# Layer 2's messages as two 12-bit float32r parts instead of three bfloat16 parts, with a newly made order of the work

## The chip, the cores and the metric

The kernel runs on one core of one Trainium2 chip. The metric is the device time in microseconds, the median of several runs. Before the change it is 3668.58 us (three runs, 3664.42 to 3668.93). The profiled execution has a span of 3661.3 us.

## What is computed

Four graph layers in a row work on 64 graphs of 256 nodes with 256 features, and each layer has the form x = x + layer(relu(layernorm(x)), adj). Layer 0 is attention with 8 heads under an adjacency mask, layer 1 a graph attention whose softmax runs over the rows, layer 3 one with 4 heads. Layer 2, in which the change lies, is a gated graph network of three iterations:

```python
A = (adj != 0).astype(x.dtype)
h = x
for i in range(3):
    m = einsum('bnd,de->bne', h, weight[i])
    aggr = einsum('bst,bsd->btd', A, m)
    h = gru_cell(aggr, h, w_ih, w_hh, b_ih, b_hh)
```

Everything is float32. A holds zeros and ones only.

## The kernel before

The graphs are taken in 32 pairs. A tile of a pair has 128 partitions and four token blocks t (graph g = t // 2, half c = t % 2) of 256 features. Transposed, as hT, it has two feature halves o of 512 columns, 256 per graph. Each pair goes through layer0 to layer3, and several pairs are under way at once, so that the softmaxes of one pair (ACT, DVE and transposes through DRAM) lie beside the matmuls of another.

The program order of all engines is made on the host by `Plan`. Each piece of work is a `Task`, added with the engines it may take, its assumed duration, the buffers it reads, writes and claims, and a latency for transfers. `Plan.order` is a list scheduler: of the tasks that are ready it takes the one that could begin first by the assumed durations, and of equal ones the one with the smallest key. Before, the key was made of the pair, times PERIOD, and of one number per layer for PE (ON_PE), for SP (ON_SP) and for all others. A task that may run on several engines (an eviction of PSUM by ACT or DVE, `evict`, lines 316 and 317) gets the one that the scheduler picks. Buffers come from pools (`SLOTS`: number, shape, type, and how many a younger pair has to leave free). The engines then run that fixed order, each in its own queue, with waits where one needs another's result.

Layer 2 (`layer2`) is written for this algebra: the message weight is folded into the input weights of the gates ahead of time (`giT`, line 411), so an iteration first forms the transposed sum aT = h^T A for the pair and then the gates from aT and hT.

- `messages` (before) splits h, which is float32, into three bfloat16 parts. The first is the upper half of h's own bits. L911 and L916 (both DVE, 128x1024) make the two rests, and the next part is again the upper half of each. The product at L929 multiplies each part with the 0/1 mask in bfloat16 (made at L894): 2 feature halves x 2 graphs x 3 parts x 2 token halves = 24 matmuls of 128x128 by 128x256. Two tasks, one per feature half, each fill a PSUM bank, which is evicted into aT.
- `gate` (L951) multiplies whhT with hT and giT with aT, all in float32, 512 columns a matmul. An iteration has, in this order of adding, the two hn gates (whhT alone), the messages, two r gates, two n gates (giT alone) and two z gates.
- Behind the z gates ACT (L1001) and DVE (L1006, L1011) form the new hT. For the next iteration the tokens-first h is made from it: for all pairs but the last by a DVE transpose (L621) and two transfers through DRAM, which leaves it in another order (`mixed`), for the last pair by PE transposes (L1025).

Other lines that are named below: L538 (PE transposes behind a layernorm), L513 and L519 (the normalised x, ACT or DVE), L567 (the products with wv and wo), L675 (those with wq and wk), L695 (scores of layer 0, four heads beside each other in row groups of 32), L745 (its context, in column groups of 32), L801 and L863 (products of layer 1), L1061 and L1113 (products of layer 3, the second in halves of 64 columns), L726 (scalings of the softmax rows, ACT or DVE), L994 (a subtraction on POOL or DVE).

The scheduler assumed 1.38 us for a block of 12 message matmuls and 1.72 us for two gate matmuls.

Of the kernel before, what the change touches and what calls it, by code (L numbers as in the profile page):

```python
# [10 lines left out]
BF = mybir.dt.bfloat16  # L11
I32 = mybir.dt.int32
# [22 lines left out]
class Task:  # L35
    __slots__ = ("pair", "forms", "bufs", "rank", "layer", "before", "after", "waits", "begin", "end", "engine", "latency", "rest", "key", "index")


class Plan:
# [14 lines left out]
    SPARE, GRAIN = 6, 0.001  # L54
# [4 lines left out]
    PERIOD, REST = 896, 0  # L59
    ON_PE = (-1435, -211, 9269, -4344)  # L60
    ON_SP = (6322, 2165, 5264, -1155)
    OTHERS = (224, 368, 701, 3083)

    def __init__(self, slots, spare):
        self.slots, self.spare = slots, spare
        self.pairs = []
        self.layer, self.rank = 0, None
# [4 lines left out]
    def add(self, forms, reads=(), writes=(), latency=0.0, claims=()):  # L72
# [11 lines left out]
        t.layer = self.layer  # L84
# [24 lines left out]

    def order(self):  # L110
# [11 lines left out]
        for t in reversed(every):  # L122
            t.rest = max((x.rest + 0.2 for x in t.after), default=0.0) + min(f[1] for f in t.forms) + t.latency
            base = t.rank[0] * self.PERIOD - t.rest * self.REST + t.rank[1] * 1e-4
            engine = t.forms[0][0]
            t.key = base + (self.ON_PE if engine == "PE" else self.ON_SP if engine == "SP" else self.OTHERS)[t.layer]
# [3 lines left out]
        free = {}  # L130
# [5 lines left out]
        while ready:  # L136
            best = None
            for t in ready:
                start = 0.0
                new = [b.tag for b in t.bufs if b.slot is None]  # L140
                for tag in set(new):
                    n = new.count(tag)
                    have = slots[tag]
                    if len(have) < n + (spares.get(tag, 0) if t.pair != oldest else 0):
                        break
                    start = max(start, have[n - 1][0])
                else:
                    for form in t.forms:
                        engine = form[0]
                        begin = max(start, free.get(engine, 0.0), free.get("port", 0.0) if len(form) > 3 else 0.0)  # L150
                        for x in t.before:
                            hop = self.HOP[x.engine] + (engine == "SP") * self.MARGIN if x.engine != engine else self.SAME[x.engine]
                            begin = max(begin, x.end + hop)
                        back = self.BACK.get(engine, 0.0) if len(t.forms) > 1 else 0.0
                        key = (round((begin + back) / self.GRAIN), t.key, t.index)
                        if best is None or key < best[0]:
                            best = (key, t, form, begin)
            _, t, form, begin = best
            engine, us, do = form[:3]
            ready.remove(t)  # L160
# [26 lines left out]
def tile_adj_preln_d4(  # L187
# [42 lines left out]
        "w4": (28, [P, T * D], FP, 9),  # L230
        "f3": (2, [P, T, E3], FP, 0),
        "mask": (6, [P, T * N], BF, 1),
        "ps": (8, [P, 512], FP, 2),
        "w2": (6, [P, N2], FP, 2),
        "st": (4, [P, T, 6], FP, 1),
        "mv": (4, [P, T, 2], FP, 1),
        "rs": (4, [P, 2, T], FP, 1),
        "mx": (16, [P, H0], FP, 2),
        "zs": (12, [P, H0], FP, 2),
        "rz": (12, [P, H0], FP, 2),  # L240
        "f12": (2, [P, 2, T], FP, 0),
        "rows": (3, [T * H3, P], FP, 0),
        "dst": (4, [P, T, H3], FP, 0),
        "turn": (8, [P, T * N], FP, 0),
        "turn2": (4, [P, N2], FP, 0),
        "row1": (4, [N2], FP, 0),
        "row3": (4, [H3 * N2], FP, 0),
# [62 lines left out]
    TURN = 0.118  # L310
# [168 lines left out]
    def norm_relu_T(xt, p, tokens=False):  # L479

        st, mv, rs = buf("st"), buf("mv"), buf("rs")
# [13 lines left out]
        xn, fine = w4(), plan.layer == 3 and p == B // 2 - 1  # L495
# [35 lines left out]
        for i in range(2):  # L531
# [13 lines left out]
            if tokens:  # L545
                add(evict(N2, dst, src), reads=[ps], writes=[(hT, i)])
            else:
                add(
                    [
                        (A, act(N2), lambda dst=dst, src=src: nc.scalar.activation(dst(), src(), AF.Relu)),  # L550
                        (V, dve(N2), lambda dst=dst, src=src: nc.vector.tensor_scalar_max(dst(), src(), 0.0)),
                    ],
                    reads=[ps], writes=[(hT, i)],
                )
        return (at, hT, xn) if tokens else (at, hT)
# [101 lines left out]
    def layer0(xt, p):  # L657
# [27 lines left out]
        for g in range(2):  # L685
            es, pT, mns = [w4() for hh in range(4)], [w4() for hh in range(4)], [buf("mx") for hh in range(4)]
            for ti in range(2):
# [15 lines left out]
                add((PE, 1.11, scores), reads=[qT, kT], writes=banks, claims=[*es, *mns])  # L703
                for e, b, mn in zip(es, banks, mns):
# [9 lines left out]
                    add((V, 2 * FUSED, logits), reads=[b, mb], writes=[(e, ti), (mn, ti)])  # L714
            for e, eT, mn in zip(es, pT, mns):
# [21 lines left out]
                turn(e, eT)  # L737
            psc = bank()
# [14 lines left out]
            add((PE, 1.93, context), reads=[(v, g), *pT], writes=[psc], claims=[cT])  # L753
# [12 lines left out]
    def to_all(row, src, columns, n, dsts):  # L766
# [3 lines left out]
            (PE, TURN, lambda: nc.tensor.transpose(ps()[0:n, 0:P], columns(), ident)),  # L770
# [16 lines left out]
    def layer1(xt, p):  # L787
# [21 lines left out]
        f1 = buf("w2")  # L809
        to_all(buf("row1"), f12, lambda: f12()[:, 0], T, [f1])  # L810
# [14 lines left out]
        )  # L825
        zs, mx, rz = buf("zs"), buf("mx"), buf("rz")
        for g in range(2):
# [28 lines left out]
            )  # L856
        for g in range(2):
# [32 lines left out]
    def layer2(xt, p):  # L890
        at, hT, h = norm_relu_T(xt, p, tokens=True)
        am = buf("mask")
        add(
            (V, dve2(T * N), lambda: nc.vector.tensor_scalar(am(), at().bitcast(I32), 0.0, None, ALU.not_equal), True),  # L894
            reads=[hT, at], writes=[am],
        )
# [3 lines left out]
        def upper(ap):  # L900
            return ap.bitcast(BF).rearrange("p (i h) -> p i h", h=2)[:, :, 1]

        def chunk_of(ap, mixed, t, o):
            if mixed:
                return upper(ap).rearrange("p (m x) -> p x m", x=2 * T)[:, T * o + t]
            return tok(upper(ap))[:, t, o * P : (o + 1) * P]

        def messages(h):
            rest = [w4(), w4()]
            add(  # L910
                (V, dve(T * N), lambda: nc.vector.tensor_tensor(  # L911
                    rest[0](), h(), upper(h()), ALU.subtract), True),
                reads=[h], writes=[rest[0]],
            )
            add(
                (V, dve(T * N), lambda: nc.vector.tensor_tensor(rest[1](), rest[0](), upper(rest[0]()), ALU.subtract), True),  # L916
                reads=[rest[0]], writes=[rest[1]],
            )
            aT = w4()
            for o in range(2):  # L920
                ps = bank()

                def product(o=o, ps=ps):
                    for g in range(2):
                        for i in range(3):
                            part = (h, *rest)[i]
                            for c in range(2):
                                t = 2 * g + c
                                mm(  # L929
                                    ps()[:, g * N : (g + 1) * N], chunk_of(part(), h.mixed, t, o), tok(am(), N)[:, t, :],  # L930
                                    start=i == 0 and c == 0, stop=i == 2 and c == 1,
                                )

                add((PE, 1.38, product), reads=[h, *rest, am], writes=[ps], claims=[aT])
                add(
                    evict(N2, lambda o=o: at_o(aT, o), ps),
                    reads=[ps], writes=[(aT, o)],
                )
            return aT

        for l in range(NL):
            r, hn, u = w4(), w4(), w4()

# [13 lines left out]
            for o in range(2):  # L957
# [9 lines left out]
                )  # L967
            aT = messages(h)
            both = ((whhT, hT), (giT[:, l], aT))
            for o in range(2):  # L970
# [10 lines left out]
                )  # L981
            for o in range(2):
# [14 lines left out]

            for o in range(2):
# [17 lines left out]
            h = w4()  # L1016
            if by_dma(l, p):
# [22 lines left out]
    def layer3(xt, p):  # L1040
# [15 lines left out]
        for t in range(T):  # L1056
# [10 lines left out]
            )  # L1067
        sd = [w4() for i in range(2)]
# [9 lines left out]
        for g in range(2):  # L1078
            zs, rz = buf("zs"), buf("rz")
# [25 lines left out]
            add((V, 0.18, lambda rz=rz, zs=zs: nc.vector.reciprocal(rz(), zs())), reads=[zs], writes=[rz])  # L1105
            pso, oT = bank(), buf("w2")
# [15 lines left out]
            add((PE, 1.86, product), reads=[*eT, (f, 2 * g), (f, 2 * g + 1)], writes=[pso], claims=[oT])  # L1122
            add(evict(N2, oT, pso), reads=[pso], writes=[oT])
            if not last:
# [47 lines left out]
    for p in range(B // 2):  # L1172
        plan.pair()
        plan.layer, xt = 0, buf("x")
# [6 lines left out]
        if p == 0:  # L1181
            for plan.rank, weights in ((None, weights0), (RANKS[0], weights1), (RANKS[1], weights2), (RANKS[2], weights3)):
                weights()
            plan.rank = None
        for plan.layer, layer in enumerate((layer0, layer1, layer2, layer3)):
            layer(xt, p)
        for g in range(2):
# [40 lines left out]
```

## Time and profile before

| | busy us | share of the span |
|---|---|---|
| PE, matmuls | 3600.6 | 98% |
| PE, weight loads (beside the matmuls) | 2042.1 | 56% |
| DVE | 2951.6 | 81% |
| ACT | 2587.2 | 71% |
| POOL | 428.1 | 12% |

| group | instructions | busy us |
|---|---|---|
| L951 matmuls, both operands | 4608 | 2142.5 |
| L929 matmuls | 2304 | 268.2 |
| L911 and L916, DVE | 192 | 235.7 |
| L894, the mask of layer 2, DVE | 32 | 21.9 |
| L621, DVE transposes for the next iteration | 93 | 192.5 |

In the profile an engine's busy time is the time in which one of its instructions is under way. The records of matmuls overlap, since their ends are modelled, so the distance between the starts of two matmuls is the better measure of what one of them costs. A float32 matmul appears as two records, a bfloat16 one as one record, and every record has its weight load beside it. The idle time before an instruction is given with the engine that ended it. The granted clock of TensorE is 1.00 in the middle of the run.

### The profile page before, as it was taken

Reading aid. Unit: us, or ns where it says so; the run is one execution under the profiler, and the core shown is the slowest. Engines: PE = TensorE matmul, PEld = TensorE weight load, DVE = VectorE, ACT = ScalarE, POOL = GpSimd, SP = SyncE. Lnnn points to the kernel's source line nnn. Section 1 sums busy time; section 2 is a strip of 40 time slices with the busy share of each in tenths; the row PEclk is TensorE's granted clock in tenths of the full one; section 3 lists DMA queues with packets and bytes.
Section 4 is the critical chain, followed back from the end, with each engine's and each line's share of the span. In section 5 each row is a group of like instructions: output and inputs, shape, how many; then the busy total and the mean of one; then the engine's idle time right before and its main releaser. Section 6 shows DMA issues by size and latency. Waiting matters only on the chain.

```text
span 3661.3 us, 55666 instructions
## 1 busy us (share of the span) xinstructions
PE 3600.6 (98%) x16369; PEld 2042.1 (56%) x16369; DVE 2951.6 (81%) x8204; ACT 2587.2 (71%) x6995; POOL 428.1 (12%) x455
## 2 busy tenths in 40 slices
PE   8999999999999999999999999999999999999996
PEld 5655555555555555555555555555555555555553
DVE  7886788888888888888888878888888888788655
ACT  6986566787666777667787667776667776677545
POOL 2000111101111011111011111011110011110100
PEclk9999999999999999999999999999999999999997
DMA  7863567876667866667766567766678666677433
GB/s 223 232 190 98 166 191 196 230 200 190 179 178 198 236 190 183 177 183 212 222 190 177 178 195 220 205 188 180 176 195 236 193 185 172 186 209 223 128 99 104
DMA packets 544144, 687.78 MB, mean 188 GB/s; under 512 B 86112, under 2 KB 463072, under 8 KB 543840
## 3 DMA queue, kind: packets, MB, share of 16 engines
q1 hardware_dynamic: 543840, 684.21, 66.3%
q8 instruction: 131, 2.15, 0.3%
q14 instruction: 173, 1.42, 0.1%
HBM read 394.28 MB, written 281.35 MB: 185 GB/s over the span
## 4 chain that ended last, share of the span: by engine, by line
PE 95%; DVE 2%; ACT 2%; DMA 1%; issue 0%; SPq 0%; POOL 0%; POOLq 0%; DVEq 0%; ACTq 0%
PE ps L951 53%; PE ps L929 7%; PE ps L567 6%; PE ps L675 6%; PE ps L695 4%; PE ps L1113 3%; PE ps L863 3%; PE ps L1061 3%; PE ps L745 3%; PE ps L801 3%; PE ps L538 3%; ACT w L651 1%; PE ps L411 0%; DVE w L602 0%; DVE w L644 0%
## 5 line engine op out<-in xcount | busy, mean ns | idle before, releaser
L951 PE MATMUL ps<-w,whhT 128*128 128x512 f32 x2304 | 1076.2, 596 | 1.4 <-ACT w L316 1.4
L951 PE MATMUL ps<-w,giT 128*128 128x512 f32 x2304 | 1066.3, 594 | 0.0
L651 ACT ACTIVATE w<-w,mx 128x256 f32<-128x256 f32 x1536 | 757.1, 496 | 1.5 <-DVE mx L644 1.5
L951 PEld LDWEIGHTS ps<-w,giT 128*128 128x128 f32 x2304 | 432.5, 190 | 530.6 <-issue 502.1
L951 PEld LDWEIGHTS ps<-w,whhT 128*128 128x128 f32 x2304 | 422.4, 190 | 463.9 <-issue 441.8
L602 DVE STREAM_TRANSPOSE w<-w 128x1024 f32<-128x1024 f32 x380 | 467.7, 1236 | 40.2 <-ACT w L726 29.9
L644 DVE CUSTOM_DVE_ANT_0 w<-ps,mask 128x256 f32<-128x256 f32 x1024 | 376.1, 417 | 44.2 <-PE ps L695 44.1
L316 ACT COPY w<-ps 128x512 f32<-128x512 f32 x547 | 302.7, 579 | 132.7 <-PE ps L929 52.6
L994 POOL TENSOR_TENSOR w<-w,w 128x512 f32<-128x512 f32 x95 | 131.0, 1379 | 1821.4 <-ACT w L989 1403.0
L726 ACT ACTIVATE w<-w,rz 128x256 f32<-128x256 f32 x688 | 299.5, 500 | 15.3 <-DVE rz L719 15.3
L973 ACT ACTIVATE w<-ps,brz 128x512 f32<-128x512 f32 x192 | 130.3, 679 | 252.7 <-PE ps L951 252.7
L513 ACT ACTIVATE w<-x,rs 128x256 f32<-128x256 f32 x394 | 211.2, 595 | 117.0 <-DVE rs L505 116.6
L651 ACT ACTIVATION_READ_ACCUMULATOR w<-w,mx 128x1 f32 x1536 | 290.7, 189 | 0.0
L978 DVE SCALAR_TENSOR_TENSOR w<-w,w 128x512 f32<-128x512 f32 x192 | 132.8, 692 | 181.4 <-ACT w L973 181.2
L929 PEld LDWEIGHTS <-w 128*128 128x128 bf16 x2304 | 246.3, 128 | 43.5 <-issue 28.4
L929 PE MATMUL ps<-mask,w 128*128 128x256 bf16 x2304 | 268.2, 273 | 2.2 <-DVE w L916 2.2
L989 ACT ACTIVATE w<-w,bih_sb 128x512 f32<-128x512 f32 x192 | 135.2, 717 | 166.6 <-DVE w L985 166.4
L1091 ACT ACTIVATE w<-w,f 128x256 f32<-128x256 f32 x512 | 228.5, 499 | 7.7 <-DMA w<-row 7.7
L550 ACT ACTIVATE w<-ps 128x512 f32<-128x512 f32 x187 | 104.3, 595 | 168.8 <-PE ps L538 168.8
L1001 ACT ACTIVATE w<-ps,brz 128x512 f32<-128x512 f32 x192 | 129.2, 673 | 126.7 <-PE ps L951 126.4
L486 DVE BATCH_NORM_STATS2 st<-x 128x6 f32<-128x256 f32 x512 | 189.6, 412 | 10.8 <-DMA x<-in_x_dram 7.4
L644 DVE CUSTOM_DVE_ANT_0 w<-w,mask 128x256 f32<-128x256 f32 x512 | 188.3, 420 | 9.9 <-ACT w L1091 9.9
(113 smaller groups left out, 5118.4 us busy)
## 6 DMA issues: line engine op xcount, KB each, us to landing
turn<-w SPq DMA_DIRECT2D x473, 512.0 KB
w<-turn SPq DMA_DIRECT2D x1892, 128.0 KB
w<-in_adj_dram SPq DMA_DIRECT2D x128, 512.0 KB
w<-row SPq DMA_DIRECT2D x64, 512.0 KB
x<-in_x_dram SPq DMA_DIRECT2D x64, 256.0 KB
out_dram<-x SPq DMA_DIRECT2D x64, 256.0 KB
turn<-w SPq DMA_DIRECT2D x62, 256.0 KB
w<-turn SPq DMA_DIRECT2D x248, 64.0 KB
```

The lines of the kernel that those rows point to most:

```text
L316: (A, act(n), lambda: nc.scalar.copy(dst(), src())),
L486: nc.vector.bn_stats(st()[:, t, :], tok(xt())[:, t, :])
L513: nc.scalar.activation(tok(xn())[:, t, :], tok(xt())[:, t, :], func, bias=rs()[:, 1, t : t + 1], scale=rs()[:, 0, t : t + 1])
L567: mm(ps()[:, c * D : (c + 1) * D], chunk(src, k, 2 * g + c), rhs[:, k, :], start=k == 0, stop=k == 1)
L602: add((V, dve(T * N), lambda: nc.vector.transpose(blocks(), blocks())), writes=[e])
L644: nc.vector.tensor_tensor_reduce(row, src, mask, scale, 3.0e38, ALU.add, ALU.min, mn)
L651: nc.scalar.activation(row(e, r), row(e, r), AF.Exp, bias=mn()[:, r : r + 1], scale=-1.0, accum_out=zs()[:, z0(r) : z0(r) + 1])
L675: mm(ps(), w[:, k, o * P : (o + 1) * P], wide(hT, k), start=k == 0, stop=k == 1)
L726: op(row, row, rz()[:, r : r + 1])
L929: mm(ps()[:, g * N : (g + 1) * N], chunk_of(part(), h.mixed, t, o), tok(am(), N)[:, t, :], start=i == 0 and c == 0, stop=i == 2 and c == 1,)
L951: mm(ps(), w[:, k, c0 : c0 + P], wide(src, k), start=n == 0, stop=n == 2 * len(terms) - 1)
L1091: nc.scalar.activation(dst, src, AF.Prelu, bias=f()[:, t, D + h : D + h + 1], alpha=ALPHA)
```

## The change

Layer 2 splits h into two parts: high, a copy into float32r[...], and low, h minus high, in float32r too. The sum of the two is to be as exact as three bfloat16 parts were. The mask A becomes float32r as well, in one tile per graph. The parts are made per graph, half a tile at a time: high by ACT or DVE, low by DVE. The product is now one task per graph: 2 feature halves x 2 parts x 2 token halves = 8 matmuls of 128x128 by 128x256, 16 for a pair. The scheduler assumes 0.9 us for the block of 8. The tiles come from a pool of their own, "part" (12 of half a w4 tile's size), and other pools change their sizes.

The order of the work is made anew: the keys are now one number for each stage of the program (some 60 stages and kinds of engine), and the scheduler knows four ways in which the PE array is tiled (whole, rows, columns, halves), counts 0.19 us for a change between them, and prefers among equal ones a task that stays in the present tiling. The assumed durations of the tiled products are set to what they take without the change of tiling (scores 1.11 to 0.88, context 1.93 to 1.75, layer 3's product 1.86 to 1.75).

The diff, cut to its core (the settings of plan.stage at each stage, the rest of the keys and the other durations are left out):

```diff
+FR = mybir.dt.float32r
...
-    SPARE, GRAIN = 6, 0.001
+    SPARE, GRAIN = 2, 0.001
...
-    PERIOD, REST = 896, 0
-    ON_PE = (-1435, -211, 9269, -4344)
-    ON_SP = (6322, 2165, 5264, -1155)
-    OTHERS = (224, 368, 701, 3083)
+    PERIOD = 1060
+    KEYS = {
+        ("io", "SP"): -9354, ("w", "SP"): 20782, ("w", "on"): 3959, ("w", "PE"): 40499, ("0n", "on"): 4124,
...
+    SWITCH = 0.19
+    HOLD = (0.00, 0.00, 0.00)
+    MODES = ("full", "rows", "columns", "halves")
...
+            t.key = t.rank[0] * self.PERIOD + t.rank[1] * 1e-4 + self.KEYS.get((t.stage, kind), 0.0)
...
+                    data = max(start, self.data(t, engine))
+                    begin = max(data, free.get(engine, 0.0), free.get("port", 0.0) if len(form) > 3 else 0.0)
+                    at = begin
+                    if engine == "PE":
+                        if t.mode != now:
+                            hold = self.HOLD[self.MODES.index(t.mode) - 1] if t.mode != "full" else 0.0
+                            if hold and tiled[t.mode] < 2:
+                                at = max(at, data + hold)
+                            begin = max(at, free.get("PE", 0.0) + self.SWITCH)
+                        elif t.mode != "full":
+                            key -= 1e6
...
         "x": (5, [P, T * D], FP, 0),
-        "w4": (28, [P, T * D], FP, 9),
+        "w4": (24, [P, T * D], FP, 2),
+        "part": (12, [P, N2], FR, 1),
         "f3": (2, [P, T, E3], FP, 0),
-        "mask": (6, [P, T * N], BF, 1),
+        "mask": (4, [P, T * N], BF, 0),
         "ps": (8, [P, 512], FP, 2),
-        "w2": (6, [P, N2], FP, 2),
-        "st": (4, [P, T, 6], FP, 1),
+        "w2": (4, [P, N2], FP, 2),
+        "st": (4, [P, T, 6], FP, 2),
         "mv": (4, [P, T, 2], FP, 1),
-        "rs": (4, [P, 2, T], FP, 1),
-        "mx": (16, [P, H0], FP, 2),
+        "rs": (4, [P, 2, T], FP, 0),
+        "mx": (16, [P, H0], FP, 3),
         "zs": (12, [P, H0], FP, 2),
-        "rz": (12, [P, H0], FP, 2),
+        "rz": (12, [P, H0], FP, 0),
         "f12": (2, [P, 2, T], FP, 0),
         "rows": (3, [T * H3, P], FP, 0),
-        "dst": (4, [P, T, H3], FP, 0),
-        "turn": (8, [P, T * N], FP, 0),
-        "turn2": (4, [P, N2], FP, 0),
-        "row1": (4, [N2], FP, 0),
-        "row3": (4, [H3 * N2], FP, 0),
+        "dst": (4, [P, T, H3], FP, 3),
+        "turn": (8, [P, T * N], FP, 1),
+        "turn2": (4, [P, N2], FP, 1),
+        "row1": (4, [N2], FP, 2),
+        "row3": (4, [H3 * N2], FP, 3),
...
-                add((PE, 1.11, scores), reads=[qT, kT], writes=banks, claims=[*es, *mns])
+                add((PE, 0.88, scores), reads=[qT, kT], writes=banks, claims=[*es, *mns], mode="rows")
...
-        am = buf("mask")
-        add(
-            (V, dve2(T * N), lambda: nc.vector.tensor_scalar(am(), at().bitcast(I32), 0.0, None, ALU.not_equal), True),
-            reads=[hT, at], writes=[am],
-        )
+        ams = [buf("part") for g in range(2)]
+        for g in range(2):
+            add(
+                (V, dve2(N2), lambda g=g: nc.vector.tensor_scalar(
+                    ams[g](), at()[:, g * N2 : (g + 1) * N2].bitcast(I32), 0.0, None, ALU.not_equal), True),
+                reads=[hT, at], writes=[ams[g]],
+            )
         at_o = lambda b, o: tok(b(), N2)[:, o, :]
 
 
-        def upper(ap):
-            return ap.bitcast(BF).rearrange("p (i h) -> p i h", h=2)[:, :, 1]
-
-        def chunk_of(ap, mixed, t, o):
+        def half_of(h, g):
+            if h.mixed:
+                return h().rearrange("p (x g c) -> p g x c", g=2, c=2)[:, g]
+            return h()[:, g * N2 : (g + 1) * N2].rearrange("p (x c) -> p x c", c=2)
+
+        def chunk_of(ap, mixed, c, o):
             if mixed:
-                return upper(ap).rearrange("p (m x) -> p x m", x=2 * T)[:, T * o + t]
-            return tok(upper(ap))[:, t, o * P : (o + 1) * P]
+                return ap.rearrange("p (m o c) -> p o c m", o=2, c=2)[:, o, c]
+            return ap.rearrange("p (c o m) -> p o c m", c=2, o=2)[:, o, c]
+
+        def pairs_of(ap):
+            return ap.rearrange("p (x c) -> p x c", c=2)
 
         def messages(h):
-            rest = [w4(), w4()]
-            add(
-                (V, dve(T * N), lambda: nc.vector.tensor_tensor(
-                    rest[0](), h(), upper(h()), ALU.subtract), True),
-                reads=[h], writes=[rest[0]],
-            )
-            add(
-                (V, dve(T * N), lambda: nc.vector.tensor_tensor(rest[1](), rest[0](), upper(rest[0]()), ALU.subtract), True),
-                reads=[rest[0]], writes=[rest[1]],
-            )
             aT = w4()
-            for o in range(2):
+            for g in range(2):
+                high, low = buf("part"), buf("part")
+                of = h if h.mixed else (h, g)
+                add(
+                    [
+                        (A, act(N2), lambda g=g, high=high: nc.scalar.copy(pairs_of(high()), half_of(h, g))),
+                        (V, dve(N2), lambda g=g, high=high: nc.vector.tensor_copy(pairs_of(high()), half_of(h, g)), True),
+                    ],
+                    reads=[of], writes=[high], claims=[low],
+                )
+                add(
+                    (V, dve(N2), lambda g=g, high=high, low=low: nc.vector.tensor_tensor(
+                        pairs_of(low()), half_of(h, g), pairs_of(high()).bitcast(FP), ALU.subtract), True),
+                    reads=[of, high], writes=[low],
+                )
                 ps = bank()
 
-                def product(o=o, ps=ps):
-                    for g in range(2):
-                        for i in range(3):
-                            part = (h, *rest)[i]
+                def product(g=g, ps=ps, high=high, low=low):
+                    for o in range(2):
+                        for i, part in enumerate((high, low)):
                             for c in range(2):
-                                t = 2 * g + c
                                 mm(
-                                    ps()[:, g * N : (g + 1) * N], chunk_of(part(), h.mixed, t, o), tok(am(), N)[:, t, :],
-                                    start=i == 0 and c == 0, stop=i == 2 and c == 1,
+                                    ps()[:, o * N : (o + 1) * N], chunk_of(part(), h.mixed, c, o), tok(ams[g](), N)[:, c, :],
+                                    start=i == 0 and c == 0, stop=i == 1 and c == 1,
                                 )
 
-                add((PE, 1.38, product), reads=[h, *rest, am], writes=[ps], claims=[aT])
-                add(
-                    evict(N2, lambda o=o: at_o(aT, o), ps),
-                    reads=[ps], writes=[(aT, o)],
+                add((PE, 0.9, product), reads=[high, low, ams[g]], writes=[ps], claims=[aT])
+                add(
+                    evict(N2, lambda g=g: tok(aT(), N2)[:, :, g * N : (g + 1) * N], lambda ps=ps: tok(ps(), N)),
+                    reads=[ps], writes=[(aT, g)],
```

## The prediction, made before the result was known

> **What bounds the kernel now.** I read the page's busy shares and its chain first.
>
> ```profile
> PE 3600.6 (98%) x16369; PEld 2042.1 (56%) x16369; DVE 2951.6 (81%) x8204; ACT 2587.2 (71%) x6995; POOL 428.1 (12%) x455
> ...
> PE 95%; DVE 2%; ACT 2%; DMA 1%; issue 0%; SPq 0%; POOL 0%; POOLq 0%; DVEq 0%; ACTq 0%
> PE ps L951 53%; PE ps L929 7%; PE ps L567 6%; PE ps L675 6%; PE ps L695 4%; PE ps L1113 3%; PE ps L863 3%; PE ps L1061 3%; PE ps L745 3%; PE ps L801 3%; PE ps L538 3%; ACT w L651 1%; PE ps L411 0%; DVE w L602 0%; DVE w L644 0%
> ```
>
> PE is 95% of the chain, and L929, the line that the change rewrites, is 7% of it by itself. A busy PE can still hide stalls, so next the busy time of the middle of the run (its columns: stretch, length, then PE, PEld, DVE, ACT, POOL busy with counts, granted clock, DMA share, GB/s) and what PE waited for in the same stretch:
>
> ```profile
> 300.00:3400.00 3100.00, 3098.18 (x14014) 1749.86 (x14013) 2547.21 (x7022) 2218.87 (x5999) 373.72 (x390) 1.00 0.68 192
> ```
>
> ```profile
> PE ps L929 <- DVE w L916: 1.6, 2, 0.8
> PE ps L1113 <- DMA w<-turn: 0.2, 1, 0.2
> ```
>
> PE waits 1.8 us in 3100. So a microsecond taken off PE's stream there is a microsecond off the time, and the vector work of the change counts only if it begins to delay PE. All other idle PE time stands at the ends: some 21 us before 300 us and 32 us after 3400 us. Third, the price of one matmul. The ends of matmuls are modelled, so I use the distance between starts, in the timeline of PE:
>
> ```profile
> 1817.89 1.88 PE L951 MATMUL ps<-w,whhT 128*128 128x512 f32 x4
> 1819.61 2.78 PE L929 MATMUL ps<-mask,w 128*128 128x256 bf16 x24
> 1822.23 1.04 PE L538 MATMUL ps<-ident,w 128*128 128x128 f32 x8
> 1823.10 1.88 PE L951 MATMUL ps<-w,whhT 128*128 128x512 f32 x4
> ...
> 1858.02 1.88 PE L951 MATMUL ps<-w,giT 128*128 128x512 f32 x4
> 1859.83 1.15 PE L695 MATMUL ps<-w,w 32*128 32x256 f32 x16
> 1860.91 1.99 PE L951 MATMUL ps<-w,whhT 128*128 128x512 f32 x4
> 1862.73 1.88 PE L951 MATMUL ps<-w,giT 128*128 128x512 f32 x4
> ```
>
> L929: 24 matmuls from 1819.61 to 1822.23, 2.62 us or 109.2 ns each. Its neighbours run at their own pace (L951 429 ns a record), so no time is lost at its borders. L695 shows what a change of the array's tiling costs: the L951 ahead takes 1.81 us, not 1.72, L695 itself 1.08, where 16 in groups of four beside each other at 216 ns are 0.86, and the L951 behind 1.82. That is 0.09 + 0.22 + 0.10 = 0.41 us for two switches, 0.2 each.
>
> [...] the trace's bf16 loads on L929 are 128 ns in the mean, f32 ones 190, so float32r may pay the slow load. [...] L916 takes 1.234 us for 1024, so halving the elements is what helps.
>
> **The change part by part.**
> Matmuls. Before, 24 per layer and pair (2 column halves, 2 graphs, 3 parts, 2 chunks), after, 16 (2 parts), over 3 x 32 = 96 such stages: 2304 to 1536, all of 256 columns. The float32r duration is unknown. Lower bound: 109.2 ns[...]. Upper: 216 ns, what one f32 record of 256 columns takes (L863 in the timeline: 16 in 3.56 us less a switch). I take the lower, for two reasons. [...] And the code's own cost for the block of 8 is 0.9 us, 112.5 ns each, in a table whose other entries fit the trace (1.38 for 12 bf16 against 1.31; 1.72 for a gate's four records against 1.72). Slow weight loads hide: f32 loads of 128 columns keep up with L538's 109 ns pace in the timeline, and behind the last of them a load of 190 ns for L951 begins just 107 ns ahead of its matmul. Saved on the path: 768 x 0.1092 = 83.9 us (with 112.5 ns: 79).
>
> Order. In the new order of instructions PE changes tiling 489 times, against 501: 12 x 0.2 = 2.4 us. The planner now knows this cost but finds little to join.
>
> DVE and ACT. Gone: L911 (117.3), L916 (118.4) and the mask L894 (21.9), 257.6 us of DVE. New: 192 low parts at half of L916's size, 0.69 us (the 128x512 tensor-tensor ops of L994), 132 us; masks of 4 bytes, 64 at 0.35 to 0.6, about 30; high parts, placed in the new order 159 on ACT at 0.58 (copies of 512, L316; 92 us) and 33 on DVE at 0.66 (22 us). The order also moves 53 evictions (35 us), some 36 subtractions of L994 (25 us) and 8 others (6) to DVE and a few scalings away from it (-31). DVE: -257.6 + 184 + 66 - 31 = about -39, 2913 us, 81% of a shorter span; ACT about +97, 75%. Neither lies on the path: DVE already kept pace at 2547 of 3100 us.
>
> The new wait. A product waits for high (ACT, queued among exponentials of 0.5 us) and then low (DVE): 0.58 + 0.69 and hops, where it waited for two DVE ops of 1.23. In the new order I counted the PE work between the release of a product's inputs and the product, with these durations and empty queues: at least 4 us in the middle of the run, mostly over 18. Behind the product the gates of L951 begin with whhT, 1.72 us that need no message, which covers the eviction of 0.58. Of the other edges on PE, those under 1 us of room are as many as before (159 against 144), but a handful in the first half (layer 1's product L863 behind its softmax) come out 1 us short. Before had none short and stalled for 1.8 us; I give 3 us.
>
> Buffers. w4 goes from 28 to 24, mask from 6 to 4, w2 from 6 to 4; 12 half-size parts come. Layer 2 no longer takes two w4 a stage for its rests, so this is even: no cost.
>
> Ends. The new SP order puts ten loads of x (2.6 MB) and some of adj ahead of wq to wo. At the page's 223 GB/s wq lands near 13 us, and before, its first product starts at 9.99: +3 us, partly made up later. At the end the last pair has no other pair beside it, and the hn gates (3.4 us), which stood behind the transposes L1025 and covered part of the message chain, now stand ahead of them: eviction, high and low are bare, 2 us in part. Together +5.
>
> Sum: 3668.6 - 83.9 - 2.4 + 3 + 5 = 3590.
>
> **The rivals.**
> A, float32r streams at f32's pace: 1536 x 216 = 332 us against 252, +80: 3668.6 + 80 - 2 + 5 = 3752, slower. [...] Against: [...] the code's 0.9.
> B, the order becomes the bound: with DVE at 81% and ACT at 75% a late high or low, or a gate whose hT comes three vector ops after the last (0.68 + 0.69 + 0.69, room nearly none in the new order in every second pair), stops PE. One DVE operation of 0.69 us in two of three of the 96 stages is 44 us: 3590 + 44 = 3634, still faster. For it: room fell for the norm's transposes behind layers 0 and 1. Against: the same shares did not stop PE before.
> C, a weight load that shows half: 130 ns each, 200 us against 252, 3622.
>
> **How the numbers follow.** Main case 0.75 (3568 to 3612), A 0.09, B 0.12, C 0.04. Range 3566 to 3640: the main case, B and C; below, the ends' 53 us of idle could shrink by 20. Left out is A and the bad tail of B. Faster 0.88, within 0.2% (7 us) 0.02, slower 0.10, A and an unlucky order.
>
> **What would show it.** The product's group should have 1536 records, 109 to 113 ns between starts, so some 170 us; PE busy about 3515; PE's waits in the middle a few us; L951 unchanged at 429 ns. Starts 216 ns apart, or two records a product, would be A. Waits of L951 or the product on DVE or ACT of tens of us would be B. The first wq product near 13 us and more idle in the last 60 us would confirm the ends.

## The result, and the profile after

The changed kernel takes 3688.74 us (four runs, 3687.54 to 3691.11) against 3666.50 us for the kernel before on the same chips: a ratio of 1.0061, 95% interval 1.0047 to 1.0076. It is 0.6% slower; the forecast was 3590 us, 2% faster, with a range of 3566 to 3640.

First the page of the kernel after: busy times, the start of the chain by engine and line, and the rows of the rewritten product.

```profile
PE 3640.1 (99%) x15601; PEld 2103.4 (57%) x15601; DVE 2898.0 (79%) x8293; ACT 2689.2 (73%) x7161; POOL 393.2 (11%) x419
...
PE 90%; ACT 5%; DMA 2%; DVE 2%; SPq 1%; issue 1%; POOL 0%; DVEq 0%; ACTq 0%
...
L984 PE MATMUL ps<-part,part 128*128 128x256 f32 x1536 | 341.2, 371 | 1.7 <-DVE part L969 0.8
L984 PEld LDWEIGHTS ps<-part,part 128*128 128x128 f32 x1536 | 310.4, 279 | 31.3 <-issue 12.6
```

There are 1536 products, as counted, each one record with one weight load. Still their busy time is 341 us, where the 2304 of before had 268. PE is as busy as ever, so the time did not go into waits. The middle of the run and PE's waits in it (the columns are those of the same stretch above) say the same:

```profile
300.00:3400.00 3100.00, 3095.03 (x13131) 1784.24 (x13130) 2473.35 (x7029) 2284.57 (x6080) 337.68 (x349) 1.00 0.67 189
```

```profile
PE ps L788 <- DMA w<-turn: 2.1, 3, 1.1
PE ps L1007 <- DVE w L1071: 1.9, 2, 1.0
PE ps L577 <- ACT w L552: 0.5, 3, 0.2
PE ps L984 <- ACT part L968: 0.4, 1, 0.4
```

4.9 us of waits in 3100, 1.8 before. So the price of a product it is. Two blocks in the timeline of PE, the first from the first iteration of a pair, the second from a later one:

```profile
952.46 1.04 PE L577 MATMUL ps<-ident,w 128*128 128x128 f32 x8
953.25 1.20 PE L984 MATMUL ps<-part,part 128*128 128x256 f32 x8
954.28 0.27 PE L813 MATMUL ps<-ident,dst 128*16 128x128 f32 x1
...
1834.79 1.88 PE L1007 MATMUL ps<-w,whhT 128*128 128x512 f32 x4
1836.10 4.18 PE L984 MATMUL ps<-part,part 128*128 128x256 f32 x16
1840.21 1.93 PE L788 MATMUL ps<-w,w 128*32 128x256 f32 x32
```

The first block of 8 takes 1.03 us to the next group. In the second, the four gates need 1.72 us, so the 16 products have from 1836.51 to 1840.21, 3.70 us, or 231 ns each. Over the whole trace the median distance between the starts of two neighbouring products is 120 ns in the first iteration and 233 ns in the second and third of the pairs 0 to 30, and the weight loads last 190 and 330 ns. In the last pair it is 120 ns in all three iterations. What differs is the order in which h lies. In the first iteration, and in the whole last pair, it is tokens first as PE and ACT left it, and the 128 columns of a weight load lie side by side. Elsewhere it comes back through DRAM in the `mixed` order, the parts keep that order in pairs, and `chunk_of` takes every fourth value: the columns of a weight load are 16 bytes apart.

The first iteration and the last pair make 544 products, the others 992. By these distances they cost 544 x 0.120 + 992 x 0.233 = 296 us, where those of before cost 2304 x 0.1092 = 252 us: +45 us. PE's listed waits fell from 54.5 us to 42.4 (the ends: 20.6 to 18.4 before 300 us, 32.1 to 19.1 after 3400 us), and 12 changes of tiling fewer are worth 2.4 by the forecast's estimate. Together +30; the profiled spans differ by 26.4 us (3661.3 to 3687.7). The other 4 us fit the granted clock of TensorE, here for the runs before and after:

```profile
core 0: 3661.3 us, clock 0.993
core 0: 3687.7 us, clock 0.996
```

In the stretches where the clock was 0.5, PE was busy for 23 us before and for 16 us after. The transposes of 128 columns (L577) stood 213 ns apart there after the change, in the median, and 109 ns at a clock of 1.00. At half the pace that is a loss of 12 and 8 us, an estimate from the clock records of the two traces.

### The profile page after: what moved, and what is told of

Read it like the earlier page. It is cut to its first block, busy times and chain, and to the rows that moved or that the text cites. A ratio compares the mean times of both kernels' runs of the same rounds, so it can differ in the third digit from the quotient of the medians.

```text
span 3687.7 us, 54450 instructions
## 1 busy us (share of the span) xinstructions
PE 3640.1 (99%) x15601; PEld 2103.4 (57%) x15601; DVE 2898.0 (79%) x8293; ACT 2689.2 (73%) x7161; POOL 393.2 (11%) x419
## 4 chain that ended last, share of the span: by engine, by line
PE 90%; ACT 5%; DMA 2%; DVE 2%; SPq 1%; issue 1%; POOL 0%; DVEq 0%; ACTq 0%
PE ps L1007 50%; PE ps L984 8%; PE ps L715 6%; PE ps L607 6%; PE ps L736 3%; PE ps L1177 3%; PE ps L1122 3%; PE ps L788 3%; PE ps L577 3%; PE ps L844 3%; PE ps L909 2%; ACT w L691 2%; DMA w<-turn 1%; ACT w L768 1%; ACT w L1154 0%
## 5 line engine op out<-in xcount | busy, mean ns | idle before, releaser
L354 ACT COPY w<-ps 128x512 f32<-128x512 f32 x500 | 285.4, 582 | 239.1 <-PE ps L984 81.0
L684 DVE CUSTOM_DVE_ANT_0 w<-ps,mask 128x256 f32<-128x256 f32 x1024 | 366.1, 419 | 63.1 <-PE ps L736 60.6
L984 PE MATMUL ps<-part,part 128*128 128x256 f32 x1536 | 341.2, 371 | 1.7 <-DVE part L969 0.8
L984 PEld LDWEIGHTS ps<-part,part 128*128 128x128 f32 x1536 | 310.4, 279 | 31.3 <-issue 12.6
L768 ACT ACTIVATE w<-w,rz 128x256 f32<-128x256 f32 x740 | 319.1, 499 | 4.7 <-DVE rz L761 4.7
L552 ACT ACTIVATE w<-x,rs 128x256 f32<-128x256 f32 x430 | 227.8, 592 | 89.7 <-DVE rs L544 88.3
L538 POOL TENSOR_SCALAR rs<-mv 128x4 f32<-128x4 f32 x129 | 41.1, 319 | 1738.6 <-DVE mv L527 1184.8
L684 DVE CUSTOM_DVE_ANT_0 w<-w,mask 128x256 f32<-128x256 f32 x512 | 198.0, 426 | 36.1 <-ACT w L1154 36.0
L1017 ACT ACTIVATE w<-ps,bhn 128x512 f32<-128x512 f32 x184 | 125.5, 682 | 121.2 <-PE ps L1007 115.3
L1053 POOL TENSOR_TENSOR w<-w,w 128x512 f32<-128x512 f32 x65 | 84.0, 1293 | 1192.9 <-ACT w L1048 749.5
```

Source lines behind the costliest of these rows:

```text
L354: (A, act(n), lambda: nc.scalar.copy(dst(), src())),
L552: nc.scalar.activation(tok(xn())[:, t, :], tok(xt())[:, t, :], func, bias=rs()[:, 1, t : t + 1], scale=rs()[:, 0, t : t + 1])
L684: nc.vector.tensor_tensor_reduce(row, src, mask, scale, 3.0e38, ALU.add, ALU.min, mn)
L768: op(row, row, rz()[:, r : r + 1])
L984: mm(ps()[:, o * N : (o + 1) * N], chunk_of(part(), h.mixed, c, o), tok(ams[g](), N)[:, c, :], start=i == 0 and c == 0, stop=i == 1 and c ...
```

## Experiments

The theory: a float32r operand whose columns lie 16 bytes apart is read at about half the pace (a load of 330 ns in place of 190), and this shows since the matmul of 256 columns, 120 ns behind the short load, is too short to hide it. The rivals: float32r itself is slow, or the h from DRAM; the stream and not the load; the new order. Up to and including "The operands changed places", every kernel keeps the order of PE's instructions as it is after the change, since no assumed duration is touched.

**Weights side by side.** Only the views through which the parts are written and read differ:

```diff
-                return h().rearrange("p (x g c) -> p g x c", g=2, c=2)[:, g]
-            return h()[:, g * N2 : (g + 1) * N2].rearrange("p (x c) -> p x c", c=2)
+                return h().rearrange("p (m o g c) -> p g c o m", o=2, g=2, c=2)[:, g]
+            return h()[:, g * N2 : (g + 1) * N2].rearrange("p (c o m) -> p c o m", c=2, o=2)
...
-            if mixed:
-                return ap.rearrange("p (m o c) -> p o c m", o=2, c=2)[:, o, c]
             return ap.rearrange("p (c o m) -> p o c m", c=2, o=2)[:, o, c]
...
-            return ap.rearrange("p (x c) -> p x c", c=2)
+            return ap.rearrange("p (c o m) -> p c o m", c=2, o=2)
```

> The two parts are written chunk by chunk, so that the 128 columns of every weight load lie side by side, in the second and third iteration too; the order of the work and all else as after the change. Theory 1 (a float32r weight load whose columns lie 16 bytes apart is slow and shows): all L984 products at 120 ns between starts, weight loads 190 ns, 1024 x 113 = 116 us less, 3689 - 116 = 3573 us, faster than both kernels. Theory 2 (float32r itself, or the token order in which h comes back through DRAM, is slow, not the step of the weights): spacing stays 233 ns in these iterations, 3689 us.

Measured: 3625.05 us, ratio to before 0.9885 (0.9869 to 0.9902), faster than both. The products and their loads, and the two casts, in the groups by line:

```profile
L982 PE MATMUL ps<-part,part 128*128 128x256 f32 x1536 | 238.2, 304 | 9.8 <-DVE part L972 7.7 <-ACT part L966 1.0 <-DVE part L967 0.8
L982 PEld LDWEIGHTS ps<-part,part 128*128 128x128 f32 x1536 | 199.5, 191 | 46.7 <-issue 20.6 <-DVE part L972 11.3 <-DVE mx L684 2.5
L972 DVE TENSOR_TENSOR part<-w,part 128x512 fp32r<-128x512 f32 x192 | 184.6, 987 | 29.6 <-ACT part L966 27.5 <-DMA w<-turn 0.5 <-DMA w<-row 0.3
L966 ACT CAST part<-w 128x512 fp32r<-128x512 f32 x159 | 149.8, 975 | 8.6 <-DMA w<-turn 7.9 <-DMA row<-rows 0.6
```

Loads are 191 ns in the mean and the distance is 120 ns in all iterations: theory 1 holds, and h's way through DRAM is not the cause. But 116 us were expected (112 with the count of 992) and 64 came. PE's busy time fell by 90 us (3640.1 to 3550.4), and its idle time rose by 20 us: the casts, which now pick single values 32 bytes apart out of `mixed`, went from 650 to 975 ns on ACT and from 734 to 987 on DVE, and the product waits for L972, the low part.

**The first iteration 16 bytes apart too.** The parts are written as (m o c) in all iterations.

```diff
-            return ap.rearrange("p (c o m) -> p o c m", c=2, o=2)[:, o, c]
+            return ap.rearrange("p (m o c) -> p o c m", o=2, c=2)[:, o, c]
...
-            return ap.rearrange("p (x c) -> p x c", c=2)
+            return ap.rearrange("p (m o c) -> p c o m", o=2, c=2)
```

> The opposite: the parts are written with 16 bytes between the columns of a weight load in the first iteration too. Theory 1: the 512 products of the first iteration go from 120 to 233 ns, 58 us more, 3747 us. Theory 2: the first iteration's h does not come through DRAM and stays at 120 ns, 3689 us.

Measured: 3770.61 us in one run. All products, those of the last pair too, stand at 233 or 234 ns, and their loads are 328 ns in the mean:

```profile
L982 PEld LDWEIGHTS ps<-part,part 128*128 128x128 f32 x1536 | 373.0, 328 | 31.1 <-issue 9.3 <-ACT w L768 2.3 <-DVE mx L684 2.2
```

The first iteration's h never went through DRAM; giving it the layout gives it the price. The time is 24 us above the 3747 of the estimate; the casts took 1160 and 1178 ns in the mean here, which may be part of it.

**8 bytes apart.** The parts are written as (o m c), so that the two token halves lie side by side and a load takes every second value.

```diff
-                return ap.rearrange("p (m o c) -> p o c m", o=2, c=2)[:, o, c]
+            return ap.rearrange("p (o m c) -> p o c m", o=2, c=2)[:, o, c]
...
-            return ap.rearrange("p (x c) -> p x c", c=2)
+            return ap.rearrange("p (o m c) -> p c o m", o=2, c=2)
```

> The parts are written with 8 bytes between the columns of a weight load, in all three iterations. If the load slows with the step, it is between 190 and 330 ns and the spacing between 120 and 233, near 3630 us; if any gap costs the whole, 233 ns everywhere, 3747 us; if only a large step costs, 120 ns, 3573 us. Theory 2: 3689 us.

Measured: 3627.04 us, 120 ns in all iterations, loads 196 ns. The casts are as slow as with the weights side by side, 998 and 996 ns in the mean. A weight load is hardly longer at 8 bytes (196 ns against 190) and is 140 ns longer at 16 (330 ns).

**512 columns streamed.** The strided weights of the change, with both graphs' masks streamed in each product.

```diff
-                                    ps()[:, o * N : (o + 1) * N], chunk_of(part(), h.mixed, c, o), tok(ams[g](), N)[:, c, :],
+                                    ps(), chunk_of(part(), h.mixed, c, o), ams[g](),
```

> Each message product streams the masks of both graphs, 512 columns in place of 256, into a whole bank (the second feature half overwrites the first, so the sums are not those of the layer). The weights are as after the change. Theory 1 (the weight load sets the pace, the stream is hidden behind it): the strided products stay near 233 ns, the contiguous ones go from 120 to 216 ns, 512 x 96 = 49 us more, 3738 us. If the stream sets the 233 ns: 466 and 240 ns, 300 us more, 3989 us.

Measured: 3759.20 us. Twice the columns take the strided products from 233 to 237 ns and the contiguous ones from 120 to 230 ns, in the median. The block shown above, now with 512 columns:

```profile
1868.21 1.88 PE L1007 MATMUL ps<-w,whhT 128*128 128x512 f32 x4
1869.53 4.32 PE L984 MATMUL ps<-part,part 128*128 128x512 f32 x16
1873.78 1.93 PE L788 MATMUL ps<-w,w 128*32 128x256 f32 x32
```

From 1869.93 to 1873.78 it takes 3.85 us, where it took 3.70 with half the columns. So behind 16-byte weights the stream of 256 columns is hidden altogether (233 ns against 237 with twice the columns), and the load of 330 ns sets the pace. The run also answers the rate of the stream: 230 ns for 512 columns is near twice the 109.2 ns that 256 bfloat16 columns took before. Rival A of the forecast, half that rate, is out.

**Pairs, placed well.** Values are read in pairs, as the change does, and the pair is written whole to where the load takes every second value; in the first iteration the parts stay side by side.

```diff
-                return h().rearrange("p (x g c) -> p g x c", g=2, c=2)[:, g]
+                return h().rearrange("p (m o g c) -> p g m o c", o=2, g=2, c=2)[:, g]
...
-                return ap.rearrange("p (m o c) -> p o c m", o=2, c=2)[:, o, c]
+                return ap.rearrange("p (o m c) -> p o c m", o=2, c=2)[:, o, c]
...
+            if mixed:
+                return ap.rearrange("p (o m c) -> p m o c", o=2, c=2)
             return ap.rearrange("p (x c) -> p x c", c=2)
```

> The parts are read and written in pairs of neighbouring values, as the change does it, but the pairs are placed so that the columns of a weight load lie 8 bytes apart (side by side in the first iteration). Products at 120 ns as with contiguous weights, and casts of 0.65 us on ACT and 0.73 us on DVE as after the change, not the 0.98 and 0.99 us that single values 32 bytes apart took. Theory 1a (what the contiguous version lost against its 3573 us are waits for its slow casts): 3689 less 303 - 190 = 113 us, some 3580 us. Rival 1b (the order has no room whatever the casts take): 3610 to 3625 us as with contiguous weights.

Measured: 3597.73 us, ratio 0.9815 (0.9801 to 0.9830), the fastest of all. In the groups by line:

```profile
L986 PE MATMUL ps<-part,part 128*128 128x256 f32 x1536 | 234.1, 302 | 2.5 <-ACT part L970 1.0 <-DVE part L971 0.8 <-DVE part L976 0.4
L986 PEld LDWEIGHTS ps<-part,part 128*128 128x128 f32 x1536 | 198.6, 194 | 36.6 <-issue 20.7 <-DVE mx L684 2.3 <-ACT part L970 1.8
L976 DVE TENSOR_TENSOR part<-w,part 128x512 fp32r<-128x512 f32 x192 | 135.7, 734 | 16.0 <-ACT part L970 13.6 <-DMA w<-turn 1.6
L970 ACT CAST part<-w 128x512 fp32r<-128x512 f32 x159 | 99.7, 658 | 10.7 <-DMA w<-turn 9.8 <-DMA row<-rows 0.6
```

The same 16 products between the same neighbours as in the timeline above:

```profile
1793.56 1.88 PE L1009 MATMUL ps<-w,whhT 128*128 128x512 f32 x4
1794.87 2.48 PE L986 MATMUL ps<-part,part 128*128 128x256 f32 x16
1797.28 1.93 PE L788 MATMUL ps<-w,w 128*32 128x256 f32 x32
```

From 1795.28 (the gates' start plus 1.72) to 1797.28 is 2.00 us, 125 ns each, where it was 3.70 us. The casts are back at 658 and 734 ns, the product waits 2.5 us for them in place of 9.8, and 27 of the 52 us that the contiguous version lacked are there. So its slow casts did cost time (1a). About 18 us against the 3580 of the estimate are still missing: PE is idle 54 us of 3592.9, 6.5 us more than after the change, and of the 112 us by which the products became cheaper (296 - 184) 101 show in PE's busy time.

**The operands changed places.** The mask is the weight, the parts stream, 16 bytes from column to column where h is mixed.

```diff
-                                    ps()[:, o * N : (o + 1) * N], chunk_of(part(), h.mixed, c, o), tok(ams[g](), N)[:, c, :],
+                                    ps()[:, o * N : (o + 1) * N], tok(ams[g](), N)[:, c, o * P : (o + 1) * P],
+                                    part().rearrange("p (m o c) -> p c o m", o=2, c=2)[:, c] if h.mixed else tok(part(), N)[:, c],
```

> The two operands of the message product change places: the mask, whose columns lie side by side, is loaded as weights, and the parts, 16 bytes from column to column in two of three iterations, stream (the sums come out untransposed, so the result is not the layer's). Theory 1 (the step costs only in the weight load): 120 ns everywhere, 3600 us or less. If a stream with 16-byte steps is slowed as the load is: 233 ns in these iterations, 3689 us.

Measured: 3699.46 us; 120 ns in the first iteration, 233 ns in the others, while the weight loads are back at 201 ns in the mean. The same block and the loads:

```profile
1844.22 1.88 PE L1008 MATMUL ps<-w,whhT 128*128 128x512 f32 x4
1845.54 4.29 PE L984 MATMUL ps<-part,part 128*128 128x256 f32 x16
1849.76 1.93 PE L788 MATMUL ps<-w,w 128*32 128x256 f32 x32
```

```profile
L984 PEld LDWEIGHTS ps<-part,part 128*128 128x128 f32 x1536 | 270.8, 201 | 55.4 <-issue 21.0
```

My theory that the step costs only in the load was wrong: a stream of 256 such columns is as slow. Two more runs with other columns of the same tiles followed:

```diff
-                                    part().rearrange("p (m o c) -> p c o m", o=2, c=2)[:, c] if h.mixed else tok(part(), N)[:, c],
+                                    part().rearrange("p (x c) -> p c x", c=2)[:, c] if h.mixed else tok(part(), N)[:, c],
```

> Mask as weights, parts streaming, as in the swapped kernel, but the stream reads the columns 8 bytes apart in two of three iterations (the same tile, other columns; the sums come out untransposed). If 8 bytes cost a stream as little as they cost a weight load: 120 ns everywhere and some 100 us less than the 3699 us of the stream with 16-byte steps, 3600 us. If a stream slows at any gap: 233 ns, 3699 us.

```diff
-                                    part().rearrange("p (m o c) -> p c o m", o=2, c=2)[:, c] if h.mixed else tok(part(), N)[:, c],
+                                    part().rearrange("p (m k o c) -> p c o k m", k=2, o=2, c=2)[:, c] if h.mixed else tok(part(), N)[:, c],
```

> The same with the streamed columns 32 bytes apart (64 of them, then the 64 between). If the cost grows with the step: over 400 ns a product, some 3860 us. If 16 bytes is where it stops growing: 233 ns, 3699 us.

Measured: 3697.47 us and 227 ns with 8 bytes, 3683.00 us and 218 ns with 32 bytes, against 233 ns with 16. For the stream each of the three gaps costs nearly the double, and the larger ones no more. So the gaps that slow the stream are not those that slow the load. For 128 weights 8 bytes are nearly free (196 against 190 ns); for 256 streamed columns they are not (227 against 120 ns).

**The order.** The change moves two things at once, so I set the rules of order back: keys per layer, no tilings, the old reserves and assumed durations, with the pools of after the change, since the parts need the room. One reserve stayed new: a younger pair has to leave 2 of the w4 tiles free, where it was 9. Of the edit only the key is shown.

```diff
-            t.key = t.rank[0] * self.PERIOD + t.rank[1] * 1e-4 + self.KEYS.get((t.stage, kind), 0.0)
+            t.key = t.rank[0] * 896 + t.rank[1] * 1e-4 + (
+                (-1435, -211, 9269, -4344) if engine == "PE" else (6322, 2165, 5264, -1155) if engine == "SP" else (224, 368, 701, 3083))[at]
```

> The messages of the change with the rules of order of before: the keys per layer, no tilings, the old assumed durations and reserves; the sizes of the pools stay as after the change, since the parts need the room. If the new order is worth its 12 switches and the 13 us less of PE waits: 3689 + 15 = 3704 us. If it is worth nothing: 3689 us. If the change's loss is the order's: 3640 us or less.

> The pairs placed 8 bytes apart, under the rules of order of before. Products 120 ns. If the order counts for some 15 us: 15 us above the same messages in the new order, 3595 us. If the old order with fewer w4 tiles starves PE: 3630 us and waits of PE on DMA or DVE.

Measured: 3892.76 us (ratio 1.0619, 1.0603 to 1.0634) with the messages of the change, 3807.68 us (1.0391, 1.0374 to 1.0408) with the well placed pairs. Both far above every expectation. The middle of the run with the first of them, and the longest waits of PE in it:

```profile
300.00:3400.00 3100.00, 3004.37 (x12526) 1713.78 (x12526) 2386.54 (x6778) 2148.94 (x5693) 371.62 (x370) 0.99 0.64 181
```

```profile
PE ps L911 <- ACT w L894: 14.9, 7, 5.0
PE ps L1009 <- ACT w L356: 14.4, 10, 7.1
PE ps L609 <- ACT w L356: 12.3, 5, 7.0
```

96 us of idle PE in the middle, spread over many lines. This is not all of the 204 us. The page of the run and its clock:

```profile
PE 3711.8 (95%) x15601; PEld 2124.9 (55%) x15601; DVE 2925.6 (75%) x8402; ACT 2641.3 (68%) x7009; POOL 448.4 (12%) x459
```

```profile
core 0: 3891.0 us, clock 0.976
```

In the whole run PE is idle for 179 us against 48 after the change, and it is busy for 72 us more with the same work. Its granted clock is 0.976 against 0.996: it was busy for 129 us at a clock of 0.5, where it was 16. At half the pace that is worth an estimated 57 of the 72 us; the other 15 are open. So the old rules starve PE here. Whether the smaller pools do this or the reserve of w4, no run separates. Either way the old rules do not cure the loss of the result: with these pools they make it larger. The layout is worth 85 us under this order too (3892.76 to 3807.68). The other way round, the new keys with the three bfloat16 parts and w4 at 28 (the code of the messages is that of before, and the reserve stays at 2):

```diff
-        "w4": (24, [P, T * D], FP, 2),
-        "part": (12, [P, N2], FR, 1),
+        "w4": (28, [P, T * D], FP, 2),
```

> The new keys, tilings, reserves and assumed durations with the three bfloat16 parts of before (w4 back at 28, since the float32r pool is gone; mask and w2 at 4 as after the change). If the new order alone is worth its 12 fewer switches and the 13 us less of PE waits: 3666 - 15 = 3651 us. If it is worth nothing by itself: 3664 us. If keys found for other durations starve PE under these: over 3680 us with PE waits in the middle.

Measured: 3745.62 us (1.0218, 1.0203 to 1.0234), with 40 us of idle PE in the middle. And the pairs with the scheduler told the measured durations. The product is shown; the cast on ACT went from 0.48 to 0.66 us and the low part from 0.60 to 0.73:

```diff
-                add((PE, 0.9, product), reads=[high, low, ams[g]], writes=[ps], claims=[aT])
+                add((PE, 0.97, product), reads=[high, low, ams[g]], writes=[ps], claims=[aT])
```

> The pairs placed 8 bytes apart, with the scheduler told the measured durations: 0.97 us for a block of 8 products, 0.66 us for the cast on ACT, 0.73 us for the low part. If the waits that are left (some 20 us outside the two ends) come from these wrong durations: 3585 us. If the keys, found for the old durations, matter more: 3598 us or above.

Measured: 3645.19 us (0.9939, 0.9922 to 0.9956), 47 us above the same pairs with the wrong durations, with no change in the work itself; the middle has 35 us of idle PE in place of 11, and the granted clock is 0.991 in place of 0.996. A likely reading of these four runs is that the keys fit the durations and pools with which they came; it is not shown by itself. What the new order is worth with the old messages cannot be read from these runs; it stays open.

## Why the prediction was wrong

**What bounds the kernel** was right. PE is the bound before and after, and the time followed PE's stream: in the middle of the run it waits 1.8 us before and 4.9 after.

**Matmuls: the step that failed.** The count was right (2304 to 1536), and so was bfloat16's pace for the stream: 512 columns took 230 ns, near twice the 109.2 ns of 256 in bfloat16. The step was "I take the lower", 109.2 ns, an estimate, since the trace of before holds no float32r, and within it "slow weight loads hide". That was shown for f32 loads whose columns lie side by side, on L538 and L951 (142 and 190 ns in the mean), and carried over to loads with a 16-byte step, which I had in the diff (`chunk_of` with `mixed`) and did not price. Side by side a load takes 190 ns, begins as the matmul before it begins, and the product stands at 120 ns; 16 bytes apart it takes 330 ns and the product waits for it, 233 ns. So the term was not -83.9 but 296 - 252 = +45 us. Of this miss of 129 us, 992 x 113 = 112 us are the step of the weights, shown by putting them side by side, and 1536 x 11 = 17 us are the 120 in place of 109. Of these 17 us no run shows the cause; that the difference does not vanish at 512 columns (230 ns against 2 x 109.2 = 218) speaks against the load.

Why did the kernel before not pay? Its weights were bfloat16 32 bytes apart in the same iterations, and its loads did get longer, 143 ns against 98 in the first iteration. But the product stood at 109 ns in all three, so the longer load was hidden. I read only the mean of 128 ns, and that mean held the warning.

**Rivals.** C had the mechanism, a weight load that shows, at 130 ns where it is 233 for two products in three, and a chance of 0.04. A had about the right pace for these two thirds and the wrong reason. B did not come in the middle of the run.

**Order, DVE and ACT, the new wait.** 489 changes of tiling, as counted. DVE came to 2898 us (2913 forecast), ACT to 2689 (2587 + 97 = 2684). High and low delayed PE's products by 1.7 us in all: hidden, as said. "I give 3 us" for the middle was 3.1.

**Ends.** The start was right in its detail (the first wq product at 12.32 us, against 9.99) and wrong in sum: the waits before 300 us fell by 2 us, and those after 3400 us by 13, where I had +5 for both. Most of it is one wait at the end: layer 3's product (L1113 before, L1177 after) waited 15.0 us for its transposes through DRAM before and 2.3 after. No run shows why. The forecast also had no term for the granted clock at the two ends.

## What to carry to other kernels

Before an operand is widened from two to four bytes, look at how far apart its columns lie, on the load and on the stream, and price the load with that step: here the bfloat16 loads of 143 ns, 32 bytes apart, hid behind matmuls of 109 ns, and the float32r loads of 330 ns, 16 bytes apart, did not (233 ns between products in place of 120). The layout is chosen where the operand is written, and the instruction that writes it should move runs of values that lie side by side on both sides (here pairs: 0.66 us a cast on ACT, against 1.13 with single values read 32 bytes apart). And a mean over instructions of one line is to be split by what they read: 128 ns here was 98 and 143.

## What the runs showed of the hardware that I had not expected

- A float32r weight load of 128 columns: 190 ns side by side, 196 ns 8 bytes apart, 330 ns 16 bytes apart.
- A float32r stream of 256 columns behind hidden loads: 120 ns side by side, 227 ns 8 bytes apart, 233 ns at 16, 218 ns at 32. Why 8 bytes cost the stream so much and the load so little, no run shows.
- Casts of 512 values to float32r on ACT, in the median: 1.13 us when single values are read 32 bytes apart and written side by side, 1.14 when they are read side by side and written 16 bytes apart (first iteration of the run with 16 bytes everywhere), 1.16 with both. With pairs read and written it was 0.66, and with side-by-side reads and writes 8 bytes apart 0.68. So one bad side was enough (1.13 or 1.14 us), and a second added little (1.16). DVE's low part goes the same way (1.09, 1.12, 1.14, 0.69, 0.69). No run shows the cause.
- The runs with much idle PE were also granted less clock: 0.996 in the mean with 48 us of idle PE (after the change), 0.988 with 105 us (new order with the old messages), 0.976 with 179 us (old order). At a clock of 0.5 the 128-column transposes L577 stood 213 ns apart in place of 109 (after the change). An order that starves PE paid here twice, in idle time and in pace.
